# Shorter lead for the samples of a deformable convolution, own tiles for three copies, and x loaded in single chunks

## The chip, the cores and the metric

The kernel runs on one core of one Trainium2 chip. The metric is the device time of one execution in microseconds (us). TensorE (PE in the profile, PEld for its weight loads), VectorE (DVE), ScalarE (ACT) and GpSimd (POOL) compute; SyncE (SP) issues most DMA transfers. Each engine works through its own queue of instructions in order, and engines wait for one another through semaphores. A Tile framework decides the order within each engine when the kernel is built, from the dependencies and from how many buffers a pool has.

## The reference

The input is x, 4 images of 1024 channels and 56 x 56 pixels, in float32. Two bottleneck layers follow each other. What matters here is the first:

```
r = relu(conv1x1(x, w1))                       # 1024 -> 256 channels
off = conv3x3(r, w_off)                        # 18 offsets for each pixel
ys, xs = own place + tap's step + offsets      # 9 taps for each pixel
sampled = bilinear gather of r at (ys, xs)     # 256 channels x 9 taps
r = relu(sum over taps of w2[tap] @ sampled)   # 256 -> 256
x1 = relu(x + conv1x1(r, w3))                  # 256 -> 1024, the "third product"
```

The second layer is a bottleneck of 1x1, 3x3 and 1x1 convolutions with batch norms, again with a residual sum. It starts inside the first layer's stretch with its own 1x1 product of x1 and goes on after it.

## The kernel before

**Blocks and taps.** For the sampling, the 3136 pixels of an image are cut into seven blocks (`j` = 0 to 6) of 512, 512, 512, 512, 384, 384 and 320 pixels. A block has nine taps (`k` = 0 to 8). A tap's pixels go in tiles of 128, so the first four blocks have four tiles for each tap, the others three. The list `taps` has 4 x 7 x 9 = 252 entries, and the main loop (lines 784 to 824 before) walks over it.

**One tap.** `sample` (L469) makes a tap's samples tile by tile. GpSimd gathers, for 128 pixels, four neighbours of 256 channels each into a tile `g` (L475, 512 KB; eight such tiles). ScalarE multiplies the first neighbour with its weight into a tile `s` (L485), and VectorE adds the other three (L487, three instructions). `turn` (L497) transposes the `s` tiles on TensorE into two PSUM banks (L512), copies them out on ScalarE (L518), and VectorE makes sums and differences of the halves (L520 to L522), for a product of 2 x 2 blocks in seven instead of eight multiplications. `tap` (L528) does the seven products on TensorE (L540) into banks that sum over the nine taps. A float32 matrix product shows as two MATMUL records in the trace.

**The end of a block.** After k = 8, ScalarE copies the sums out (L555 to L559): two into `r2`, and three into tiles p3, p5 and p4. VectorE combines them (L561 to L567), ScalarE applies the relu. The three p tiles are taken from the pool under the tag `s`, so they are three of the twelve buffers that the samples also go round in. A new tile takes the buffer that was given out twelve tiles earlier, and its first writer waits until the readers of that buffer are done: for a sample tile these readers are the transposes of L512.

**The order of the loop.** Before the loop, the samples of the first three taps are written down, and tap 0 is turned. In iteration i the loop writes down `turn` of tap i + 1, `sample` of tap i + 3, and `tap` of i. Then it fills up with other matrix work by a budget: pieces of `stage_a` (the first product of the next image, its offsets, and the table for the gathers), `stage_b` (positions and weights of a block) or `stage_c` (below). `due` (L763) names the one place before the end of an image at which all of the next image's first part must have been written down, since the next image's samples come right after: (j, k) = (6, 5) before. The framework may move instructions within an engine from this order, but not past their dependencies.

**The third product.** `stage_c` (L574) takes a finished block `r2`. For each of eight chunks of 128 channels, `wide` (L593) copies x into a PSUM bank on ScalarE (L595), adds the product with w3 on TensorE (L600), and ScalarE applies the relu (L611); `first` multiplies the result for the second layer (L626). x comes by DMA from SyncE (L587) into tiles `xr`: before, two tiles of two chunks each (512 KB for 512 pixels). The first two loads are issued at the start of a stage, the load of chunks k + 3 and k + 4 after the copy of an odd chunk k.

Of the kernel before, what the change touches and what calls it, by code (L numbers as in the profile page):

```python
# [14 lines left out]
CB = 256  # L15
# [45 lines left out]
def deform_bottleneck_then_bn_bottleneck(  # L61
# [107 lines left out]
    with ExitStack() as l0:  # L169
# [3 lines left out]
        wa = l0a.enter_context(tc.tile_pool(name="w_l0a", bufs=1, side="right"))  # L173
        xin = l0a.enter_context(tc.tile_pool(name="xin", bufs=4, side="right"))
        worka = l0a.enter_context(tc.tile_pool(name="work_a", bufs=1, side="right"))
        xres = l0.enter_context(tc.tile_pool(name="xres", bufs=2))
        gat = l0.enter_context(tc.tile_pool(name="gat", bufs=8))
        work = l0.enter_context(tc.tile_pool(name="work", bufs=2))
        w3p = l0.enter_context(tc.tile_pool(name="work3", bufs=3))
# [53 lines left out]


        def load_zeros():
            zero = w3p.tile([128, CB], F32, tag="s", name="zero", bufs=12)
            nc.vector.memset(zero[: PW + 2], 0.0)
            for n in range(N):
                for corner, s in enumerate((0, PW)):
                    first_row = PW - s + TPAD  # L240
                    for r0, r1 in ((0, first_row), (first_row + H * PW, TROWS)):
                        if r1 > r0:
                            nc.sync.dma_start(tables[n][r0:r1, corner, :], zero[: r1 - r0, :])
# [225 lines left out]
        def sample(n, j, k):  # L469

            size = SIZES[j]
            for t in range((size + 127) // 128):
                m = min(128, size - t * 128)
                g = gat.tile([128, 4 * CB], F32, tag="g", name=f"g_{n}_{j}_{k}_{t}")
                nc.gpsimd.indirect_dma_start(  # L475
                    out=g[:m],
                    out_offset=None,
                    in_=tables[n].rearrange("r q c -> r (q c)"),
                    in_offset=bass.IndirectOffsetOnAxis(
                        ap=idxs[n, j][:m, t, k : k + 1], axis=0  # L480
                    ),
                )
                s = w3p.tile([128, CB], F32, tag="s", name=f"s_{n}_{j}_{k}_{t}", bufs=12)
                wt = wts[n, j][:m, :, t, k : k + 1]
                nc.scalar.activation(s[:m], g[:m, 0:CB], AF.Copy, scale=wt[:, 0])  # L485
                for corner in range(1, 4):
                    nc.vector.scalar_tensor_tensor(  # L487
                        s[:m],
                        g[:m, corner * CB : (corner + 1) * CB],
                        wt[:, corner],  # L490
                        s[:m],
                        ALU.mult,
                        ALU.add,
                    )
                samples[n, j, k, t] = s
# [32 lines left out]
        def tap(n, j, k):  # L528
            size = SIZES[j]
            half = size // 2  # L530
            if k == 0:
                accs[n, j] = [
                    pst.tile([128, 512], F32, tag=f"tap{i}", name=f"acc2_{n}_{j}_{i}")
                    for i in range(4)
                ]
            sts = turned.pop((n, j, k))
            sums = [accs[n, j][i // 2][:, i % 2 * half : (i % 2 + 1) * half] for i in range(7)]
            for i, (a, b) in enumerate(PRODUCTS):

                nc.tensor.matmul(  # L540
                    sums[i],
                    w2[:, a, k],
                    sts[:, b, :half],
                    start=(k == 0 and i % 2 == 0),
                    stop=(k == TAPS - 1),
                    skip_group_check=True,
                )
            if k == TAPS - 1:
                r2 = work.tile([128, KB, 512], F32, tag="r2", name=f"r2_{n}_{j}", bufs=R2S)
                p3, p5, p4 = (  # L550
                    w3p.tile([128, CB], F32, tag="s", name=f"p{i}_{n}_{j}", bufs=12)[:, :half]
                    for i in (3, 5, 4)
                )
                r = [[r2[:, o, e * half : (e + 1) * half] for e in range(2)] for o in range(KB)]
                nc.scalar.copy(r2[:, 0, :size], accs[n, j][0][:, :size])  # L555
                nc.scalar.copy(p3, sums[2])
                nc.scalar.copy(p5, sums[3])
                nc.scalar.copy(r2[:, 1, :size], accs[n, j][2][:, :size])
                nc.scalar.copy(p4, sums[6])  # L559
                add = nc.vector.tensor_add  # L560
                add(r[1][0], r[1][0], r[0][0])  # L561
                add(r[1][1], r[1][1], r[1][0])
                add(r[0][0], r[0][0], r[0][1])
                add(r[0][1], r[1][0], p5)
                add(r[0][1], r[0][1], p3)
                add(r[1][0], r[1][1], p4)
                add(r[1][1], r[1][1], p5)  # L567
                for o in range(KB):
                    nc.scalar.activation(
                        r2[:, o, :size], r2[:, o, :size], AF.Relu, bias=col("a_b2", o)  # L570
                    )
                r2s[n, j] = r2

        def stage_c(n, j):  # L574

            b = n * NJ + j
            size = SIZES[j]
            blk = slice(STARTS[j], STARTS[j] + size)
            r2 = r2s.pop((n, j))
            xrs, x1ts, y1s = {}, {}, []  # L580

            def load(kk):
                if kk < KC:
                    xr = xres.tile([128, 2, 512], F32, tag="xr", name=f"xr_{b}_{kk}")[
                        :, :, :size
                    ]
                    nc.sync.dma_start(xr, x_v[n, :, kk : kk + 2, blk])  # L587
                    xrs[kk] = xr

            def wide(k):  # L593
                z = psz.tile([128, 512], F32, tag="z", name=f"pr_{b}_{k}")[:, :size]
                nc.scalar.copy(z, xrs[k - k % 2][:, k % 2, :])  # L595
                if k % 2:
                    load(k + 3)
                yield
                for h in range(KB):
                    nc.tensor.matmul(  # L600
                        z,
                        w3[:, h, k * 128 : (k + 1) * 128],
                        r2[:, h, :size],
                        start=False,
                        stop=(h == KB - 1),
                        skip_group_check=True,
                    )
                yield KB * size
                x1t = w3p.tile([128, 512], F32, tag="x1t", name=f"x1t_{b}_{k}", bufs=X1S)
                x1ts[k] = x1t = x1t[:, :size]  # L610
                nc.scalar.activation(x1t, z, AF.Relu, bias=col("a_b3", k))  # L611
                nc.sync.dma_start(x1_v[n, :, k, blk], x1t)

            def first(h, part):
                z = psz.tile([128, 512], F32, tag="z", name=f"acc3_{b}_{h}_{part}")[:, :size]
                if part == 0:
                    y1s.append(
                        w3p.tile([128, 512], F32, tag="y1", name=f"y1_{b}_{h}", bufs=2)[:, :size]
                    )
                    begin_with(z, col("b1", h))  # L620
                else:
                    nc.scalar.copy(z, y1s[h])  # L622
                yield
                for i in range(KC // 2):
                    k = part * KC // 2 + i
                    nc.tensor.matmul(  # L626
                        z,
                        c1w[:, k, h * 128 : (h + 1) * 128],
                        x1ts[k],
                        start=False,  # L630
                        stop=(i == KC // 2 - 1),
                        skip_group_check=True,
                    )
                    if i % 2:
                        yield 2 * size
                nc.scalar.copy(y1s[h], z)  # L636
                if part == 1:
                    nc.vector.bn_stats(y1_stats[:, h, b * 6 : b * 6 + 6], y1s[h])
                    nc.sync.dma_start(y1_v[n, :, h, blk], y1s[h])

            jobs = (
                [wide(k) for k in range(KC // 2 + 1)]
                + [first(h, 0) for h in range(KB)]
                + [wide(k) for k in range(KC // 2 + 1, KC)]
                + [first(h, 1) for h in range(KB)]
            )
            load(0)
            load(2)
            yield from run(jobs)

        def last_positions(n):
# [110 lines left out]

        def due(n, j, k):  # L763

            if n + 1 == N or (j, k) != (NJ - 1, TAPS - 4):
                return False
            return (first_ones and first_ones[0][0] == n + 1) or {stage, upcoming} & set(running)

# [8 lines left out]
            return None  # L777

        ahead = iter(taps)
        for _ in range(3):  # L780
            sample(*next(ahead))
        turn(*taps[0])
        stage, upcoming, extra, budget = None, None, None, 0.0
        for i, (n, j, k) in enumerate(taps):
# [608 lines left out]
```

## Time and profile before

The time is 2967.17 us, the median of three runs (2964.87 to 2967.61). The profiled execution has a span of 2972.2 us.

| engine | busy us | share of the span |
|---|---|---|
| PE (matrix products) | 2815.1 | 95% |
| PEld (weight loads) | 1937.6 | 65% |
| DVE | 2078.7 | 70% |
| ACT | 1511.0 | 51% |
| POOL | 1171.9 | 39% |

The samples are made between about 147 and 2164 us of the span (first L485 and last L487); before lies the first product of image 0, after it the rest of the second layer. In this stretch the DMA engines are busy for about 88% of the time, most of it with the 900 gathers: their queue took 43.2% of the engines' time over the whole span.

How to read the lines: in the table of waits, a line names the engine and line that waited, what it waited for, and the total us, the number of waits and the longest one. In a timeline, a line has the start in us, the length in us, the engine, the line, the operation, its tiles with shapes, and the number of instructions merged; in brackets stands the engine's idle time just before and what ended it. A busy engine is not always an engine that works at its peak, and idle time costs something only where TensorE waits for it in the end.

### The profile page before, as it was taken

What the parts mean: (1) busy time and instruction counts of PE and PEld (TensorE: products, weight loads), DVE (VectorE), ACT (ScalarE), POOL (GpSimd) and SP (SyncE); (2) the same over time, 40 slices, a digit from 0 to 9 for tenths busy, and PEclk for the clock granted to TensorE, in tenths of its full rate; (3) what the DMA queues carried; (4) which work ended last, traced back from release to release, by engine and by line L of the source; (5) the groups of instructions that cost most, each with busy time, mean ns of one, the idle gap of its engine ahead of it and who ended that gap; (6) DMA issues with size and microseconds to landing.
All of it is one profiled execution on the core that took longest, in us unless ns stands there. A gap on an engine that the chain in (4) does not pass through costs nothing.

```text
span 2972.2 us, 38613 instructions
## 1 busy us (share of the span) xinstructions
PE 2815.1 (95%) x12001; PEld 1937.6 (65%) x12001; DVE 2078.7 (70%) x4961; ACT 1511.0 (51%) x3069; POOL 1171.9 (39%) x998
## 2 busy tenths in 40 slices
PE   9889999989998989998999989999989998999999
PEld 4455666767665666665666556666669998965554
DVE  2188887788786768776777887778749887334444
ACT  2145664655654545554564555566552544434444
POOL 0066565565565457555555565555500000000000
PEclk9999999999999999999999999999999999999999
DMA  7699998899988889888988989998840110139997
GB/s 247 198 357 360 337 346 294 299 323 340 350 315 303 305 266 326 296 335 299 336 295 260 322 301 343 330 337 297 289 139 23 46 45 24 54 128 322 305 308 261
DMA packets 335311, 792.10 MB, mean 267 GB/s; under 512 B 31448, under 2 KB 181504, under 8 KB 335104
## 3 DMA queue, kind: packets, MB, share of 16 engines
q0 software_dynamic: 127296, 462.48, 43.2%
q1 hardware_dynamic: 177328, 275.77, 28.0%
q10 hardware_dynamic: 30480, 51.39, 4.6%
q8 instruction: 94, 1.54, 0.2%
q14 instruction: 113, 0.93, 0.1%
HBM read 640.68 MB, written 143.48 MB: 264 GB/s over the span
## 4 chain that ended last, share of the span: by engine, by line
PE 57%; DMA 13%; DVE 6%; ACT 4%; issue 3%; SPq 0%; POOL 0%; ACTq 0%; POOLq 0%; DVEq 0%
PE acc L540 11%; PE pf L1161 11%; DMA g<-table,idxs 11%; PE q L988 7%; PE acc L626 7%; PE pr L600 6%; PE acc L312 4%; PE stp L512 3%; DVE s L487 3%; PE acc_g L1211 2%; DMA xr<-in_x_dram 2%; PE b L988 2%; PE pm L361 1%; ACT s L485 1%; PE tp L1192 1%
## 5 line engine op out<-in xcount | busy, mean ns | idle before, releaser
L475 POOL DMA_INDIRECT g<-table,idxs x900 | 1161.4, 1290 | 990.3 <-DVE s L487 326.8
L487 DVE SCALAR_TENSOR_TENSOR s<-g,wts,s 128x256 f32<-128x256 f32 (+1 forms) x2700 | 1165.2, 477 | 239.3 <-ACT s L485 138.4
L540 PE MATMUL acc<-sts,w 128*128 128x256 f32 (+2 forms) x3528 | 737.2, 358 | 7.7 <-DVE sts L520 2.6
L540 PEld LDWEIGHTS acc<-sts,w 128*128 128x128 f32 x3528 | 609.4, 193 | 65.5 <-ACT sts L518 4.4
L485 ACT ACTIVATE s<-g,wts 128x256 f32<-128x256 f32 x900 | 429.8, 508 | 416.0 <-DMA g<-table,idxs 327.1
L600 PE MATMUL pr<-r,w 128*128 128x512 f32 (+2 forms) x896 | 373.4, 553 | 39.6 <-ACT pr L595 34.7
L626 PE MATMUL acc<-x1t,c1w 128*128 128x512 f32 (+2 forms) x896 | 363.0, 547 | 14.5 <-ACT acc L622 12.8
L312 PE MATMUL acc<-xt,w 128*128 128x448 f32 x896 | 357.7, 546 | 11.4 <-DMA xt<-in_x_dram 11.4
L512 PEld LDWEIGHTS stp<-ident,s 128*128 128x128 f32 (+1 forms) x1800 | 215.0, 143 | 166.0 <-issue 86.8
L1161 PE MATMUL pf<-y,c3w 128*128 128x448 f32 x844 | 317.4, 539 | 0.0
L512 PE MATMUL stp<-ident,s 128*128 128x128 f32 (+1 forms) x1800 | 258.4, 277 | 39.2 <-ACT off L438 20.3
L600 PEld LDWEIGHTS pr<-r,w 128*128 128x128 f32 x896 | 164.9, 193 | 185.9 <-issue 86.4
L518 ACT COPY sts<-stp 128x512 f32<-128x512 f32 (+2 forms) x504 | 242.9, 529 | 60.3 <-PE stp L512 50.2
L626 PEld LDWEIGHTS acc<-x1t,c1w 128*128 128x128 f32 x896 | 168.8, 192 | 156.6 <-issue 90.4
L312 PEld LDWEIGHTS acc<-xt,w 128*128 128x128 f32 x896 | 169.0, 193 | 149.2 <-issue 140.8
L1325 DVE SCALAR_TENSOR_TENSOR x1f<-pf,sc_bn,x1f 128x448 f32<-128x448 f32 x211 | 144.3, 684 | 172.3 <-PE pf L1161 160.1
L1161 PEld LDWEIGHTS pf<-y,c3w 128*128 128x128 f32 x844 | 160.4, 190 | 156.8 <-issue 118.4
L1333 ACT ACTIVATE x1f<-x1f,sh_bn 128x448 f32<-128x448 f32 x224 | 148.4, 667 | 173.6 <-DVE x1f L1325 172.7
L520 DVE TENSOR_TENSOR sts<-sts 128x256 f32<-128x256 f32 (+2 forms) x252 | 97.7, 388 | 165.3 <-ACT sts L518 157.5
L611 ACT ACTIVATE x1t<-pr,ch 128x512 f32<-128x512 f32 (+2 forms) x224 | 141.2, 630 | 86.5 <-PE pr L600 75.5
L522 DVE TENSOR_TENSOR sts<-sts 128x512 f32<-128x512 f32 (+2 forms) x252 | 155.4, 617 | 1.3
L636 ACT COPY y<-acc 128x512 f32<-128x512 f32 (+2 forms) x112 | 59.2, 528 | 165.6 <-PE acc L626 146.4
(221 smaller groups left out, 2421.1 us busy)
## 6 DMA issues: line engine op xcount, KB each, us to landing
xt<-in_x_dram SPq DMA_DIRECT2D x112, 448.0 KB
x1f<-x_d SPq DMA_DIRECT2D x112, 448.0 KB
out_dram<-x1f ACTq DMA_DIRECT2D x111, 448.0 KB
xr<-in_x_dram SPq DMA_DIRECT2D x64, 512.0 KB
x_d<-x1t SPq DMA_DIRECT2D x128, 256.0 KB
table<-ft SPq DMA_DIRECT2D x56, 384.0 KB
g<-table,idxs POOLq DMA_INDIRECT x900
xr<-in_x_dram SPq DMA_DIRECT2D x32, 384.0 KB
```

The costliest lines, as they stand in the source:

```text
L312: nc.tensor.matmul(acc, w1[:, k, h * 128 : (h + 1) * 128], xts[n, j, k - k % 2][:, k % 2, :], start=start, stop=(k == KC - 1), skip_group_ ...
L475: nc.gpsimd.indirect_dma_start(out=g[:m], out_offset=None, in_=tables[n].rearrange("r q c -> r (q c)"), in_offset=bass.IndirectOffsetOnAxi ...
L485: nc.scalar.activation(s[:m], g[:m, 0:CB], AF.Copy, scale=wt[:, 0])
L487: nc.vector.scalar_tensor_tensor(s[:m], g[:m, corner * CB : (corner + 1) * CB], wt[:, corner], s[:m], ALU.mult, ALU.add,)
L512: nc.tensor.transpose(banks[h][:, t * 128 : t * 128 + m], s[:m, h * 128 : (h + 1) * 128], ident[:m, :m],)
L518: nc.scalar.copy(to, banks[h][:, :size].rearrange("p (e q) -> p e q", e=2))
L522: nc.vector.tensor_sub(sts[:, 5:7, :half], sts[:, 1:4:2, :half], sts[:, 0:2, :half])
L540: nc.tensor.matmul(sums[i], w2[:, a, k], sts[:, b, :half], start=(k == 0 and i % 2 == 0), stop=(k == TAPS - 1), skip_group_check=True,)
L600: nc.tensor.matmul(z, w3[:, h, k * 128 : (k + 1) * 128], r2[:, h, :size], start=False, stop=(h == KB - 1), skip_group_check=True,)
L626: nc.tensor.matmul(z, c1w[:, k, h * 128 : (h + 1) * 128], x1ts[k], start=False, stop=(i == KC // 2 - 1), skip_group_check=True,)
L988: nc.tensor.matmul(ps[:, o].rearrange("p r c -> p (r c)"), wt, x, start=first and j == 0 and (alone or o == 0), stop=last and j == len(pai ...
L1161: nc.tensor.matmul(pz, c3w[:, h, k * 128 : (k + 1) * 128], y2[n][:, h, j * BLK : (j + 1) * BLK], start=(h == 0), stop=(h == KB - 1),)
```

## The change

Three things change in the first layer's stretch.

- Samples are made two taps ahead instead of three: two are written down before the loop, so that iteration i writes down `sample` of tap i + 2, and the samples go round in eight tiles instead of twelve. `due` names the tap k = 6 instead of 5, as the next image's samples come one tap later.
- The copies p3, p5 and p4 get a tag of their own with three tiles, and no longer take a turn in the ring of the samples.
- x for the third product is loaded by single chunks (256 KB for 512 pixels) into five tiles. The first five loads are issued at the start of the stage, and chunk k + 5 after the copy of chunk k.

The aim is to use less of the on-chip memory for samples and to spend it on loads of x that are asked for earlier and in smaller pieces.

```diff
-        xres = l0.enter_context(tc.tile_pool(name="xres", bufs=2))
+        xres = l0.enter_context(tc.tile_pool(name="xres", bufs=5))
...
-            zero = w3p.tile([128, CB], F32, tag="s", name="zero", bufs=12)
+            zero = w3p.tile([128, CB], F32, tag="s", name="zero", bufs=8)
...
-                s = w3p.tile([128, CB], F32, tag="s", name=f"s_{n}_{j}_{k}_{t}", bufs=12)
+                s = w3p.tile([128, CB], F32, tag="s", name=f"s_{n}_{j}_{k}_{t}", bufs=8)
...
                 p3, p5, p4 = (
-                    w3p.tile([128, CB], F32, tag="s", name=f"p{i}_{n}_{j}", bufs=12)[:, :half]
+                    w3p.tile([128, CB], F32, tag="p", name=f"p{i}_{n}_{j}", bufs=3)[:, :half]
                     for i in (3, 5, 4)
                 )
...
-            def load(kk):
-                if kk < KC:
-                    xr = xres.tile([128, 2, 512], F32, tag="xr", name=f"xr_{b}_{kk}")[
-                        :, :, :size
-                    ]
-                    nc.sync.dma_start(xr, x_v[n, :, kk : kk + 2, blk])
-                    xrs[kk] = xr
+            def load(k):
+                if k < KC:
+                    xrs[k] = xres.tile([128, 512], F32, tag="xr", name=f"xr_{b}_{k}")[:, :size]
+                    nc.sync.dma_start(xrs[k], x_v[n, :, k, blk])
...
-                nc.scalar.copy(z, xrs[k - k % 2][:, k % 2, :])
-                if k % 2:
-                    load(k + 3)
+                nc.scalar.copy(z, xrs[k])
+                load(k + 5)
...
-            load(0)
-            load(2)
+            for k in range(5):
+                load(k)
...
-            if n + 1 == N or (j, k) != (NJ - 1, TAPS - 4):
+            if n + 1 == N or (j, k) != (NJ - 1, TAPS - 3):
...
-        for _ in range(3):
-            sample(*next(ahead))
+        sample(*next(ahead))
+        sample(*next(ahead))
```

## The prediction

> **What bounds the kernel now.** I read the engine totals first, then the stages, then the table of waits, and last the timeline around one stall.
>
> ```profile
> PE 2815.1 (95%) x12001; PEld 1937.6 (65%) x12001; DVE 2078.7 (70%) x4961; ACT 1511.0 (51%) x3069; POOL 1171.9 (39%) x998
> ```
>
> TensorE carries the time; no other engine is near the span. The change touches only the stretch with sampling (first transpose at 148.8 us, last copy of x for the third product at 2199.2 us). In its steady part:
>
> ```profile
> 230.00:2190.00 1960.00, 1851.54 (x7901) 1257.74 (x7902) 1497.72 (x3869) 1102.49 (x2352) 1098.95 (x849) 0.98 0.88 312
> ```
>
> The columns are length, busy PE, PEld, DVE, ACT, POOL, granted clock, DMA share, GB/s. PE is idle for 1960.0 - 1851.5 = 108 us. That is the most that better feeding can give here, 3.7% of the kernel. DMA engines are 88% busy, so transfers can be late. Who waits:
>
> ```profile
> ACT s L485 <- DMA g<-table,idxs: 327.1, 217, 8.6
> POOL g L475 <- DVE s L487: 326.8, 244, 12.3
> ACT pr L595 <- DMA xr<-in_x_dram: 20.3, 8, 6.2
> ```
>
> ScalarE starts each sample tile (L485) and waits 327 us for gathered data; the gathers in turn wait 327 us for a free `g` tile. No PE line waits directly for `s`. So how does a late gather reach PE? The largest PE gap, in the timelines of ScalarE, GpSimd and TensorE:
>
> ```profile
> 892.50 0.61 ACT L595 COPY pr<-xr 128x512 f32<-128x512 f32 x1
> 900.09 0.51 ACT L485 ACTIVATE s<-g,wts 128x256 f32<-128x256 f32 x1 [6.99 <-DMA g<-table,idxs]
> 902.86 0.51 ACT L485 ACTIVATE s<-g,wts 128x256 f32<-128x256 f32 x1 [2.26 <-DMA g<-table,idxs]
> 905.21 0.59 ACT L595 COPY pr<-xr 128x512 f32<-128x512 f32 x1
> ...
> 884.07 0.94 POOL L475 DMA_INDIRECT g<-table,idxs  x1 [8.22 <-ACT sts L518]
> 888.21 6.74 POOL L475 DMA_INDIRECT g<-table,idxs  x1 [3.20 <-DVE s L487]
> ...
> 905.85 2.93 PE L600 MATMUL pr<-r,w 128*128 128x512 f32 x3 [7.99 <-ACT pr L595]
> ```
>
> ScalarE is held at `s` by a late gather, and the copy that opens the next product (L595, 905.21) stands behind it. PE stops 8 us for that copy. The sample that caused it is not needed by PE until its transposes at 926.6 us. A sample made far ahead hurts through the queue it blocks, not through its own deadline.
>
> **Which samples do this.** I gave every L485, L487 and L512 of the trace its tap by counting along its queue, then put each PE gap over 0.3 us between 230 and 2190 us to the ScalarE wait that covers it or ends within 6 us before it. The gaps sum to 104.4 us: ScalarE held at a sample of tap k=5 37.6, k=6 18.6, the seven other taps together 28.0 (of it k=3 none, k=4 1.2, so 26.8 for k=0,1,2,7,8); waiting at L595 7.0; other 13.2. ScalarE's idle time before samples shows the same: k=0,1,2 about 37 us each, k=3 1.3, k=4 3.0, k=5 102, k=6 92, k=7,8 about 42.
>
> The cause is the ring of `s`. After tap 8 of a block the kernel takes p3, p5, p4 (L551) out of the same twelve tiles. Twelve back from the samples of k=3 and k=4 then lie tiles of a tap later than otherwise, so those samples must wait for transposes one tap later. In the built order of ScalarE a tap's last sample stands on average 2.5 taps ahead of its own copies (L518) at k=0,1,2, 1.67 at k=3, 2.10 at k=4, 2.5 to 2.6 after. At k=5 the lead jumps back: the `g` tiles of k=5 are freed only by the late L487 of k=3, VectorE runs 17 of these in a row (6.80 us from 887.00), GpSimd, which sat idle, has a burst to issue, and ScalarE is already at k=5.
>
> [...] L595 ran only after the held L485. [...] the gather issue of 888.21 under the 17 L487 took 6.74 us against a median of 0.99. [...]
>
> **Part 1, own tiles for p.** It adds and removes no instruction. The delay at k=3, k=4 and the jump at k=5 vanish: in the built order of the changed kernel the lead is 1.32 to 1.54 for all nine taps. k=5 and k=6 should then behave as the undisturbed taps. These cost 26.8 / 5 = 5.4 us of PE gaps per k, so nine cost 48.2, against 37.6 + 18.6 + 28.0 = 84.2 now: **-36 us**. Bounds: nothing, if the burst only moves, and -56 us, if the gaps of k=5 and 6 go and k=3, 4 stay near zero.
>
> **Part 2, two taps ahead in eight tiles.** Same samples, same 2700 L487 of 477 ns and 900 L485 of 508 ns; they stand one tap later beside PE's order, which is otherwise nearly the same. Price: slack. From a tile's last L487 to its transpose the median is now 16.6 us, with a period of about 8 us per tap. One tap less leaves what lies between the end of the next tap's samples and this tap's transpose: median 8.4 us. After the ramp it is negative in 5 of 237 taps, 6 us in sum; if every sample were 2 us later still, 23 us; 4 us later, 78 us. About half of these come from k=2, whose next tap is the delayed k=3, which part 1 mends: without it 3, 13 and 43 us. PE would stand at L512, with its own tap and the products queued behind. I take a lateness of about 1 us: **+5 us** (6.5 without k=2); ends 3 and 43. The gathers keep their lead over L485, since a `g` tile is freed by L487 of two taps before in both kernels; at undisturbed taps 8.6 to 9.4 us pass from issue to use (least 3.7), so two taps fit in flight.
>
> In the ramp (148.8 to 230 us) the samples have 0.1 us of slack and PE waits for them already. They start as soon as their gathers land in both: 0.
>
> **Part 3, x by chunks.** The same bytes in 224 issues for 112. 112 more at 0.38 us are 43 us of SyncE's queue spread over 2000 us, beside its waits: 0. The order of waits changes: a pair k, k+1 was requested after the copy of chunk k-3; a chunk is now requested after the copy of k-5, the first five at the start of the stage. The six waits over 1.5 us at L595 lie at k=4 (2.1, 1.8, 2.4) and k=6 (2.3, 4.0, 6.2), 8 to 15 us after issue; two chunks more give about 10 us more. PE loses 7.0 us at L595: **-5 us**; ends 0 and -7.
>
> **Part 4, the forced draining before an image's end** (`due`) one tap later, and two samples ahead of the loop: the same work, within the ±2 us that I can't see: 0.
>
> Sum: -36 + 5 - 5 = -36 us, 2967 - 36 = **2931 us**.
>
> **Rivals.**
> A, a larger gain. Also the 28 us at other taps shrink, since ScalarE comes to each sample later in PE's time: -56 - 7 - 14 (half of 28) + 5 = -72, 2895 us. For it: the k=3 samples, at short lead, cost PE nothing. Against it: their gathers had a long lead then (16.6 us from issue to use), which the change doesn't give.
> B, slower: the short lead becomes the bound. With gathers landing 4 us later than now PE waits 43 to 78 us at L512, against at most -41 from parts 1 and 3; with 78, 2967 + 78 - 41 = 3004; with 60, 2986 us. For it: single waits up to 8.6 us for gathers, as long as the whole median slack; four-tile blocks have a lead of only 1.15 to 1.30. Against it: at k=3, the shortest lead today, the slack to the transpose never fell under 6.9 us.
> C, no change: the gathers' burst is replaced by the same waits spread out, because transfers at 88% busy set them; gains and the +5 cancel: 2967 us.
>
> **Chances.** Forecast 0.58, A 0.15, B 0.17, C 0.10. Faster by over 0.2% (6 us): 0.58 + 0.15 = 0.73; same: C, 0.10; slower: B, 0.17. The range takes the forecast's ends: low with all 56 + 7 us gained and the 3 us lost, about 2905; high up to C and a mild B, 2976.
>
> **What would show it.** Part 1: idle time of ScalarE before samples of k=5 and 6 falls from about 100 to about 40 us each, k=3 and 4 rise to that, and the wait for gathers falls under 300 us. Part 2: few PE gaps whose next instruction is L512 with its sample just finished; median slack near 8 us. Part 3: ScalarE's waits for `xr` near zero. Stage 230 to 2190 shorter by some 36 us, the tail after 2200 us unchanged in length. I am wrong if PE's waits for `s` exceed 40 us, or if ScalarE waits for gathers as long as before.

## The result and the profile after

The changed kernel takes 2866.52 us (median of four runs, 2858.5 to 2868.69) against 2967.39 us in the same session: a ratio of 0.9654, 95% interval 0.9632 to 0.9675. Beside later experiments it came out at 0.9644 (0.9623 to 0.9665). It is 3.5% faster, 101 us; the forecast was 36 us, with 2905 us as the lower end of its range. The direction was right and the size was not.

The engine totals and the stage from 230 to 2190 us (length, busy PE, PEld, DVE, ACT, POOL, granted clock, DMA share, GB/s):

```profile
PE 2775.4 (97%) x12001; PEld 1924.8 (67%) x12001; DVE 2070.1 (72%) x4961; ACT 1503.3 (52%) x3069; POOL 1120.8 (39%) x998
```

```profile
230.00:2190.00 1960.00, 1913.30 (x8428) 1335.29 (x8429) 1579.65 (x4034) 1134.19 (x2423) 1048.26 (x872) 0.99 0.89 316
```

In the same 1960 us PE has 8428 records instead of 7901, and 47 us without work instead of 108. (The changed kernel's last transpose starts at 2068 us, so this window takes in some of its tail too; the table further down compares like with like.) The first line says something that idle time can't: the same 12001 records of PE took 40 us less in sum (2815.1 before). The products themselves became shorter. So the forecast's ceiling, that the 108 us without work are the most that better feeding can give, was drawn too low. We come back to this.

The table of waits of the changed kernel:

```profile
DVE s L487 <- ACT s L485: 299.9, 179, 16.0
POOL g L475 <- DVE s L487: 283.5, 291, 11.1
ACT s L485 <- DMA g<-table,idxs: 149.4, 110, 8.1
ACT s L485 <- PE stp L512: 101.5, 78, 5.0
```

ScalarE's wait for gathers fell from 327.1 to 149.4 us. Its wait for a free `s` tile (for L512) rose to 101.5 us; before it was

```profile
ACT s L485 <- PE stp L512: 55.7, 36, 5.0
```

The shorter lead isn't the reason: the run with own p tiles at the old lead, below, has 100.2 us of it. PE hardly suffers from late samples in either kernel: its waits at L512 for VectorE's sums are 10.3 us before and 11.5 after. The copy of x now waits 0.4 us for its load, 20.3 before:

```profile
L592 ACT COPY pr<-xr 128x512 f32<-128x512 f32 (+2 forms) x224 | 121.4, 542 | 4.7 <-DMA xr<-in_x_dram 0.4
```

The product ahead of which PE stood for 8 us starts at 890.2 us in the changed kernel, in place of 905.85. ScalarE's timeline, and TensorE's:

```profile
885.00 0.61 ACT L592 COPY pr<-xr 128x512 f32<-128x512 f32 x1
885.51 1.32 ACT L485 ACTIVATE s<-g,wts 128x256 f32<-128x256 f32 x3
888.68 0.69 ACT L607 ACTIVATE x1t<-pr,ch 128x512 f32<-128x512 f32 x1 [1.85 <-PE pr L596]
889.40 0.59 ACT L592 COPY pr<-xr 128x512 f32<-128x512 f32 x1
...
886.77 5.31 PE L596 MATMUL pr<-r,w 128*128 128x512 f32 x12
891.92 1.04 PE L512 MATMUL stp<-ident,s 128*128 128x128 f32 x8
```

Three samples, here of tap k=4, pass in 1.32 us with their gathers landed. ScalarE then waits for PE and not the other way round, and the twelve records of L596 follow without a gap.

**Where the 101 us came from.** I added up, for the stretch from 230 us to the last transpose, PE's gaps and the time in which PE worked while the trace records a granted clock of half (0.5). What is left when gaps and half of the slow time are taken off is called the rest. Half is an estimate from the stall of the kernel before, shown further down, where a record of L600 came every 0.43 us ahead of the stall and every 0.85 to 1.01 us at that clock: it takes PE to do half as much in all such time.

| kernel | stretch us | PE gaps | at half clock | rest |
|---|---|---|---|---|
| before | 1947.0 | 106.1 | 67.7 | 1807.0 |
| changed | 1838.3 | 36.2 | 19.6 | 1792.2 |

Of the 108.7 us, 69.9 are gaps, (67.7 - 19.6) / 2 = 24 are slow clock, and 15 lie in the rest. The two profiled executions lie 108 us apart, the medians 101. The rest lies between 1791 and 1807 us in all the profiled kernels of this study, so it is the same to about 1%; the kernel before and its control with five x1t tiles, alike in time, differ by 6 us in it. After the last transpose both kernels take 795 us.

### The profile page after: what moved, and what is told of

Same layout as the page of the kernel before. It is cut to its first block, busy times and chain, and to the rows that moved or that the text cites. A ratio compares the mean times of both kernels' runs of the same rounds, so it can differ in the third digit from the quotient of the medians.

```text
span 2864.2 us, 39301 instructions
## 1 busy us (share of the span) xinstructions
PE 2775.4 (97%) x12001; PEld 1924.8 (67%) x12001; DVE 2070.1 (72%) x4961; ACT 1503.3 (52%) x3069; POOL 1120.8 (39%) x998
## 4 chain that ended last, share of the span: by engine, by line
PE 84%; DMA 7%; DVE 5%; ACT 2%; issue 2%; SPq 0%; POOL 0%; ACTq 0%; DVEq 0%; POOLq 0%
PE acc L540 19%; PE pf L1157 11%; PE pr L596 11%; PE acc L622 11%; PE acc L312 10%; PE q L984 7%; PE stp L512 6%; DMA g<-table,idxs 5%; DVE s L487 3%; PE acc_g L1207 2%; PE b L984 2%; PE pm L361 2%; PE ftp L391 1%; PE tp L1188 1%; PE pa L1157 1%
## 5 line engine op out<-in xcount | busy, mean ns | idle before, releaser
L475 POOL DMA_INDIRECT g<-table,idxs x900 | 1110.3, 1234 | 939.5 <-DVE s L487 283.5
L487 DVE SCALAR_TENSOR_TENSOR s<-g,wts,s 128x256 f32<-128x256 f32 (+1 forms) x2700 | 1173.3, 476 | 310.6 <-ACT s L485 299.9
L540 PE MATMUL acc<-sts,w 128*128 128x256 f32 (+2 forms) x3528 | 723.5, 355 | 5.3 <-ACT sts L518 4.1
L540 PEld LDWEIGHTS acc<-sts,w 128*128 128x128 f32 x3528 | 601.2, 190 | 56.3 <-ACT sts L518 7.4
L485 ACT ACTIVATE s<-g,wts 128x256 f32<-128x256 f32 x900 | 427.0, 511 | 285.7 <-DMA g<-table,idxs 149.4
L596 PE MATMUL pr<-r,w 128*128 128x512 f32 (+2 forms) x896 | 367.7, 548 | 19.6 <-ACT pr L592 12.8
L512 PEld LDWEIGHTS stp<-ident,s 128*128 128x128 f32 (+1 forms) x1800 | 212.7, 142 | 137.6 <-issue 83.4
L596 PEld LDWEIGHTS pr<-r,w 128*128 128x128 f32 x896 | 165.0, 192 | 160.6 <-issue 84.3
L512 PE MATMUL stp<-ident,s 128*128 128x128 f32 (+1 forms) x1800 | 252.2, 274 | 16.6 <-DVE s L487 11.5
L592 ACT COPY pr<-xr 128x512 f32<-128x512 f32 (+2 forms) x224 | 121.4, 542 | 4.7 <-DMA xr<-in_x_dram 0.4
```

The costliest lines, as they stand in the source:

```text
L475: nc.gpsimd.indirect_dma_start(out=g[:m], out_offset=None, in_=tables[n].rearrange("r q c -> r (q c)"), in_offset=bass.IndirectOffsetOnAxi ...
L487: nc.vector.scalar_tensor_tensor(s[:m], g[:m, corner * CB : (corner + 1) * CB], wt[:, corner], s[:m], ALU.mult, ALU.add,)
L512: nc.tensor.transpose(banks[h][:, t * 128 : t * 128 + m], s[:m, h * 128 : (h + 1) * 128], ident[:m, :m],)
L540: nc.tensor.matmul(sums[i], w2[:, a, k], sts[:, b, :half], start=(k == 0 and i % 2 == 0), stop=(k == TAPS - 1), skip_group_check=True,)
L596: nc.tensor.matmul(z, w3[:, h, k * 128 : (k + 1) * 128], r2[:, h, :size], start=False, stop=(h == KB - 1), skip_group_check=True,)
```

## The experiments

Three explanations were set against each other. **Ring**: the p tiles' turn in the samples' ring delays the samples of two taps and bunches the gathers after them. **Lead**: samples made less far ahead meet gathers that have landed. **Loads**: x in chunks asked for earlier.

**Own p tiles alone.**

```diff
-                    w3p.tile([128, CB], F32, tag="s", name=f"p{i}_{n}_{j}", bufs=12)[:, :half]
+                    w3p.tile([128, CB], F32, tag="p", name=f"p{i}_{n}_{j}", bufs=3)[:, :half]
...
-X1S = 6
+X1S = 5
```

> The kernel before with own tiles for p3, p5, p4 alone: samples still three taps ahead in twelve tiles, x by pairs. To make room the relu outputs x1t have five tiles instead of six (a control run shows that alone). Ring theory (the p tiles' turn in the ring of the samples causes the bunched gathers, the long stalls and the slow clock after them): most of the gain comes from here, 2870 to 2900 us, idle time of ScalarE before samples of k=5 and 6 falls from about 100 to 40 us each. Lead theory (samples made less far ahead let ScalarE come to them later, when the gather has landed): little, 2935 to 2967 us. Loads theory (x by chunks): 2960 to 2975 us.

Measured: 2875.85 us, 0.9664 (0.9637 to 0.9691). The control for its x1t tiles:

> Control for the run with own p tiles: the kernel before with five instead of six tiles for the relu outputs x1t, nothing else. All theories: 2967 us or up to 15 us more, as a product may wait for an output tile.

Measured: 2970.34 us, 0.9998 (0.998 to 1.0017). So three tiles of 1 KB in each partition bring all but about 0.1% of the whole gain, which is within the noise, with the lead of three taps untouched. The ring theory was right, the lead and loads theories were wrong. The waits of the run with own p tiles:

```profile
POOL g L475 <- DVE s L487: 289.0, 275, 14.1
ACT s L485 <- DMA g<-table,idxs: 164.3, 136, 7.4
...
ACT s L485 <- PE stp L512: 100.2, 72, 5.0
```

By tap, ScalarE's idle time before samples (us, from 230 us on) shows what the ring did:

| kernel | k=0 | 1 | 2 | 3 | 4 | 5 | 6 | 7 | 8 |
|---|---|---|---|---|---|---|---|---|---|
| before | 38 | 35 | 38 | 1 | 3 | 102 | 92 | 41 | 43 |
| own p alone | 33 | 31 | 35 | 16 | 17 | 29 | 29 | 27 | 29 |
| changed | 30 | 36 | 23 | 19 | 29 | 27 | 34 | 30 | 24 |
| changed, p back in the ring | 40 | 42 | 3 | 7 | 87 | 77 | 58 | 34 | 44 |

**p back in the ring, the rest of the change kept.**

```diff
-                    w3p.tile([128, CB], F32, tag="p", name=f"p{i}_{n}_{j}", bufs=3)[:, :half]
+                    w3p.tile([128, CB], F32, tag="s", name=f"p{i}_{n}_{j}", bufs=8)[:, :half]
```

> The changed kernel with p3, p5, p4 put back into the ring of the samples, now of eight tiles; two ahead and chunks of x stay. Ring theory: the dip of the lead (now at k=2 and 3) and the burst after it come back, 2910 to 2960 us, with PE also waiting for samples at the dip. Lead theory: 2870 to 2890 us. Loads theory: 2870 to 2890 us.

Measured: 2932.67 us, 0.9853 (0.9821 to 0.9885). In the last row above, the dip moved to k=2 and 3, one tap earlier as the lead is one tap shorter, and the hump to k=4 to 6. The waits for gathers doubled again:

```profile
POOL g L475 <- DVE s L487: 304.6, 294, 10.5
ACT s L485 <- DMA g<-table,idxs: 302.6, 187, 8.8
```

At the same lead, own tiles are also three more tiles in all. The total isn't what counts: the changed kernel with x by pairs, below, has eleven (eight and three) with its shorter lead, against the twelve before, and keeps the gain. Whether a shared ring with three more tiles (fifteen at three ahead, eleven at two) would do as well as own tiles was not run.

**Two taps ahead in eight tiles alone** (p in the ring, x by pairs).

```diff
-            if n + 1 == N or (j, k) != (NJ - 1, TAPS - 4):
+            if n + 1 == N or (j, k) != (NJ - 1, TAPS - 3):
...
-        for _ in range(3):
-            sample(*next(ahead))
+        sample(*next(ahead))
+        sample(*next(ahead))
...
-                s = w3p.tile([128, CB], F32, tag="s", name=f"s_{n}_{j}_{k}_{t}", bufs=12)
+                s = w3p.tile([128, CB], F32, tag="s", name=f"s_{n}_{j}_{k}_{t}", bufs=8)
...
```

> The kernel before with samples made two taps ahead in eight tiles and nothing else: p3, p5, p4 stay in that ring, x by pairs. Ring theory: like the changed kernel with the shared ring and a little worse for the waits on x, 2935 to 2965 us. Lead theory: 2870 to 2900 us. A third possibility, that the shorter lead hurts with the shared ring: over 2970 us.

Measured: 2953.93 us, 0.993 (0.9904 to 0.9957). With the shared ring, the shorter lead is a little better than the longer one, not worse. Why, these runs don't show: PE's gaps are 98.4 us, little under the 106.1 before. Against the run above, which differs from this one in x by chunks alone, it is 0.8% slower (0.993 against 0.9853, in different sessions). That is more than chunks bring elsewhere, though the two profiled executions lie only 9 us apart; this stays open.

**x by pairs again in the changed kernel** (the diff's lines on `xres` and `load` undone).

```diff
-            def load(k):
-                if k < KC:
-                    xrs[k] = xres.tile([128, 512], F32, tag="xr", name=f"xr_{b}_{k}")[:, :size]
+            def load(kk):
+                if kk < KC:
+                    xr = xres.tile([128, 2, 512], F32, tag="xr", name=f"xr_{b}_{kk}")[
...
```

> The changed kernel with x loaded by pairs into two tiles as before; two ahead in eight tiles and own p tiles stay. Ring and lead theory: waits for x of about 20 us on ScalarE come back, 2870 to 2885 us. Loads theory: 2920 us or more.

Measured: 2873.83 us, 0.9663 (0.9636 to 0.969). ScalarE's waits for x came back, with 18.9 us, and all but about 0.1% of the gain stayed: chunks don't cause most of it.

**Chunks alone in the kernel before**, with four tiles for x:

```diff
-        xres = l0.enter_context(tc.tile_pool(name="xres", bufs=2))
+        xres = l0.enter_context(tc.tile_pool(name="xres", bufs=4))
...
-                if k % 2:
-                    load(k + 3)
+                load(k + 4)
...
```

> The kernel before with x by single chunks alone, into four tiles (the same bytes as two pairs; a fifth has no room), each chunk asked for four ahead; three ahead in twelve tiles and the shared ring stay. Ring theory: ScalarE's waits for x of 20 us nearly vanish and PE's 7 us with them, 2955 to 2968 us. Loads theory (chunks cause most of the gain): under 2920 us.

Measured: 2964.83 us, 0.9976 (0.9956 to 0.9996), some 7 us. ScalarE idled 6 us before copies of x, 20 before the change. Both runs agree with the forecast's 5 us for this part. Own p alone at three ahead measured 0.9664, and own p at two ahead 0.9663, both with x by pairs. So no effect of the shorter lead shows once p has its own tiles; each interval reaches 0.27% (8 us) to either side, so 5 us could hide in it.

**Three taps ahead with everything else changed.**

```diff
-                s = w3p.tile([128, CB], F32, tag="s", name=f"s_{n}_{j}_{k}_{t}", bufs=8)
+                s = w3p.tile([128, CB], F32, tag="s", name=f"s_{n}_{j}_{k}_{t}", bufs=12)
...
-        xres = l0.enter_context(tc.tile_pool(name="xres", bufs=5))
+        xres = l0.enter_context(tc.tile_pool(name="xres", bufs=3))
...
```

> The changed kernel with samples three taps ahead in twelve tiles again, own p tiles kept; room comes from three instead of five tiles for x, each chunk asked for three ahead. If the shorter lead itself costs or gains nothing: 2862 to 2878 us. If the short lead costs the 5 us that the forecast put on it: 2858 to 2864 us. Lead theory: over 2900 us.

Measured: 2880.82 us, 0.9693 (0.9661 to 0.9725), so not faster. With three tiles for x, waits for x of 24 us came back, which muddies it; no gain from the longer lead shows.

**Added stalls**, to test the slow clock.

```diff
+            if n and k == 4:
+                nc.scalar.copy(w2[:, :5], w2[:, :5])
             tap(n, j, k)
```

> The changed kernel with 21 stalls put in: in images 1 to 3, at tap 4 of each block, ScalarE copies five sevenths of the second product's weights onto themselves (5760 columns, 5 to 6 us by the rate of its other copies), and the products that read them wait. Outputs are unchanged. Slow-clock theory (after a stall the granted TensorE clock drops to half for a while, and that costs a second time): 5 to 15 such periods more than in the changed kernel, and the stretch grows by the added PE gaps plus half of the added time at half clock. Rival (the lower clock has another cause): the stretch grows by the gaps alone, half-clock time stays near 20 us. With 60 to 120 us of gaps added: 2950 to 3020 us.

Measured: 2901.05 us, 0.9754 (0.9714 to 0.9795). The test missed its aim. PE waited for these copies only 8 times, 15.6 us in sum: in most places other products stood ahead of the waiting ones. So the 21 stalls added only 19 us of gaps (55.5 against 36.2) and 8 us at half clock. It can't tell the theories apart.

What speaks to it is a count over the traces of all fourteen profiled executions, which run much the same code, so their gaps are not independent cases. Of PE's gaps from 230 us to 2190 us, so many had a period at half clock that began in them or within 8 us after:

| gap | number | with a slow period | mean slow time, us |
|---|---|---|---|
| 1 to 2 us | 135 | 17 | 0.5 |
| 2 to 3 us | 51 | 34 | 2.8 |
| 3 to 4 us | 42 | 34 | 3.9 |
| 4 to 5 us | 29 | 29 | 4.6 |
| 5 to 9 us | 36 | 36 | 7.8 |

All 65 gaps over 4 us had the half clock. It began 1.8 to 5.4 us after the gap had begun, so the gap came first. Of the 145 periods at half clock in these stretches, 144 began in a gap of over 1 us or within 8 us after one, and they last 3.41, 6.83 or 10.24 us. The slow time in the table includes the part that falls into the gap: in the last row PE was at work in 4.5 of the 7.8 us. In these traces, then, the half clock went with idle time of PE, and not with long idle time alone: ahead of 64 of the 145 periods PE had stood for less than 3 us in the 6.8 us before. Around the 8 us stall of the kernel before, by stretches (during it, just after, later; the column with 0.86, 0.58 and 1.00 is the granted clock):

```profile
893.00:905.00 12.00, 4.86 (x15) 2.44 (x13) 6.29 (x16) 2.03 (x5) 9.56 (x9) 0.86 1.01 352
905.80:913.00 7.20, 7.15 (x20) 4.74 (x21) 2.67 (x8) 4.23 (x8) 1.88 (x2) 0.58 1.03 402
913.00:920.00 7.00, 7.00 (x24) 3.90 (x23) 4.67 (x11) 2.21 (x5) 3.81 (x4) 1.00 0.88 298
```

and TensorE's timeline there:

```profile
894.27 3.60 PE L600 MATMUL pr<-r,w 128*128 128x512 f32 x8
905.85 3.78 PE L600 MATMUL pr<-r,w 128*128 128x512 f32 x4 [7.99 <-ACT pr L595]
```

Eight records of L600 took 3.60 us ahead of the stall; four took 3.78 us after it. PE is fully busy in the second stretch, and yet these products come at about half the rate. By this reading a long stall is paid for twice. That rests on the count and the order in time; no run changed the clock by itself.

**Attempts to beat both.** More gathers in flight, with room taken elsewhere:

```diff
-        gat = l0.enter_context(tc.tile_pool(name="gat", bufs=8))
+        gat = l0.enter_context(tc.tile_pool(name="gat", bufs=9))
...
```

> The changed kernel with nine gather tiles instead of eight; room for it comes from three instead of five tiles for x, each chunk asked for three ahead. An attempt to beat it. If what is left of ScalarE's waits for gathers (149 us) comes from too few gathers in flight, these fall under 110 us and the time to 2845 to 2860 us; if the transfers themselves are the limit, 2865 us or, with waits for x coming back, up to 2880 us.

Measured: 2868.1 us, 0.9637 (0.9602 to 0.9672): waits for gathers 100.0 us, but 27.3 us for x. So the time missed the range that went with fewer waits for gathers. Then with four tiles for x and five for x1t:

> An attempt to beat the changed kernel: nine gather tiles, four tiles for x with each chunk asked for four ahead, and five instead of six tiles for the relu outputs x1t, which cost nothing in their control. With three tiles for x, nine gather tiles cut the waits for gathers from 149 to 100 us and waits of 27 us for x took the gain back. If four tiles for x keep these waits under 8 us: 2845 to 2862 us; if late gathers no longer matter to PE: 2865 us.

Measured: 2857.15 us, 0.9598 (0.9576 to 0.962), with 5.3 us of waits for x, but 127.9 us for gathers, more than the 100.0 of the run before. And with ten gather tiles (`bufs=10`, R2S = 4 in addition):

> The same with ten gather tiles; room from four instead of five tiles for finished blocks r2. If more gathers in flight go on helping: 2835 to 2858 us; if a block must wait for a free r2 tile near an image's end, 2870 us or more.

Measured: 2849.99 us, 0.9579 (0.9559 to 0.96). Beside these two ran the changed kernel itself:

> The changed kernel itself, beside the others on one chip: 2860 to 2875 us.

Measured: 2864.74 us, 0.9644 (0.9623 to 0.9665). The intervals of the ten-tile kernel and the changed one don't overlap: the kernel with ten gather tiles is some 15 us faster. Its wait for gathers is down to 63 us:

```profile
POOL g L475 <- DVE s L487: 245.2, 269, 10.1
...
ACT s L485 <- DMA g<-table,idxs: 62.6, 43, 10.2
```

Nine tiles can't be told from eight with confidence: 0.9598 reaches up to 0.962 and the changed kernel down to 0.9623, which is close to the edge, and the other run with nine measured 0.9637.

## Why the prediction was right in direction and wrong in size

**Part 1, own tiles for p.** The mechanism was right: two delayed taps, a jump in the lead at k=5, late gathers at k=5 and 6, ScalarE blocked, PE stopped behind. The run with this part alone shows it, and the one with p put back loses more than half of the whole gain. The term "-36 us" was the step that failed: the same part alone measured 0.9664, about 100 us. Its far bound of -56 us was passed too. Three things stand in its place; their sizes are from the run with own p alone against the kernel before.

- PE's gaps fell by 106.1 - 45.2 = 61 us. The forecast took k=0, 1, 2, 7 and 8 for undisturbed, with 5.4 us per tap, and left 48.2 us for nine. By the same count 27.6 us are left in the run with own p alone, and 31.5 after the whole change. So at the nine taps the gain was 57 us and not 36, as much as the far bound. The fault lies with the base of 5.4 us per tap: k=5 and 6 fell from 56.2 to 5.2 us together, not to 10.8, and the five taps themselves from 26.8 to 17.3. They were no clean base, perhaps because they too lay in a loop disturbed once per block. The gaps put down to "other" fell as well, from 13 to about 4 us.
- The slow clock was left out. 67.7 us at half clock fell to 30.2, worth 19 us by the estimate above. The profile had shown it: the forecast quotes a granted clock of 0.98 in its stage line and puts no term on it. By the count above, the cost of a gap of 4 us and more should have been its length plus half of the slow time in which PE works after it.
- 13 us lie in the rest (1807.0 against 1794.1). I can give no cause for them; 6 us of difference in the rest come about without any difference in time, as said above.

**Part 2, the shorter lead.** Priced at +5 us, it shows no effect: own p at two ahead and at three ahead are 0.9663 and 0.9664, but 5 us lie within the noise of these runs. The median slack of a tap's last sample to its transpose is about 9 us in the changed kernel (forecast near 8), and only one tap of some 240 has less than 0.3 us. One figure of the forecast is named wrongly: the leads of 2.5, 1.67, 2.10 and 1.32 to 1.54 taps are means over all tiles of a tap, not of its last tile. For last tiles alone they are 2.2 to 2.3, 1.50, 1.96 and 1.20 to 1.36, with the same dip.

**Part 3, chunks.** -5 us forecast; 0.9976 as a single edit, and ScalarE's waits for x went from 20.3 to 0.4 us. Right within what can be told. What went with these waits is how far ahead a chunk was asked for, not its size by itself: they are 24 to 27 us with single chunks three ahead (three tiles), 5 to 11 us four ahead and 0.4 us five ahead.

**Part 4 and the ramp.** Nothing was expected. The first transpose of block 1 of image 0 starts at 218.8 us before and 218.3 after, and image 1's first at 639.5 and 637.7. All the gain lies in images 1 to 3: from an image's first transpose to the next one's 509 and 521 us became 473 and 477, and image 3 went from 506 to 480 us. PE's gaps in image 0 did not fall (11 us from 230 us on before, 13 after), although ScalarE's waits before its samples of k=5 and 6 fell from 38 to 8 us. So these waits don't always reach PE; why they don't in image 0, I didn't test.

**The rivals.** B, the short lead as the bound, was refuted. A had the right sign for its doubt, that the other taps would improve too, but not its reason: they improve at the long lead as well. A's 2895 us, 72 us of gain, were still short of the measured 101; the 24 us of slow clock make up most of that. C, no change, was refuted too: the waits for gathers did not spread out, they fell by half.

**Two readings of the forecast.** The long gather issue of 6.74 us lay under the 17 L487 that ran for 6.80 us from 887.00 us. Whether VectorE's bursts lengthen gather issues was not shown: no run separates this, and from 230 to 2190 us the issues over 2 us fell from 89 to 71 with the change. That a held sample also holds what stands behind it on ScalarE carried the argument, and the stall shows it. The product that L611 reads had ended by 897.87 us (894.27 + 3.60 in TensorE's timeline above). ScalarE stood idle until 900.09 us before its first held L485, and L611 ran only after the third of them:

```profile
904.09 0.51 ACT L485 ACTIVATE s<-g,wts 128x256 f32<-128x256 f32 x1 [0.72 <-DMA g<-table,idxs]
904.51 0.67 ACT L611 ACTIVATE x1t<-pr,ch 128x512 f32<-128x512 f32 x1
```

L595 followed at 905.21 us, and PE's products at 905.85 us.

## What to carry to other kernels

A tile that lives in another purpose's ring takes a turn in it: look, at each rotation, at which reader a new tile then waits for, and at what happens when the delay ends all at once. Work done far ahead can still stop the engine that matters, through what stands behind it: here ScalarE stood 6.99, 2.26 and 0.72 us before three samples, and PE 7.99 us for the copy behind them. When PE stalls for several us, look also at the clock and the products after it. In these traces a mean granted clock of 0.98 over the stretch went with 106 us of gaps and 68 us at half clock, and 0.99 with 36 and 20 us.

## What was not expected of the hardware

The half clock with stalls, by the count above: 65 of 65 gaps over 4 us, 17 of 135 between 1 and 2 us, in 64 of 145 periods after less than 3 us of standing still in the 6.8 us before, and products of L600 that took twice as long just after the stall (four records in 3.78 us, eight in 3.60 us ahead of it). In this kernel the summed busy time of the same 12001 PE records moved by 40 us between two versions, so busy time is no constant of the work.
